# x1 transposed by DMA in 16-bit halves, attention's product moved, and a layer norm's scale folded into W1

## The chip, the cores and the metric

The kernel runs on one core of one Trainium2 chip. The metric is the device time of one execution in microseconds (us). Before the change three executions took 1932.43, 1933.75 and 1933.97 us; the median is 1933.75 us.

## What is computed

The input is src, 4 batches of 2048 rows of 256 numbers (f32). Each row is normalised (xn). Two branches work on xn, and their product is added to src.

```python
xn = layernorm(x)                                    # no scale, no shift
# branch 1: linear attention, then a two-layer network
Q, K = elu(xn @ Wq + bq) + 1, elu(xn @ Wk + bk) + 1  # 16 heads of 64
KV = einsum('bshd,bshm->bhdm', K, xn @ Wv + bv)      # sum over the rows of a batch
Z  = 1 / (einsum('bshd,bhd->bsh', Q, K.sum(axis=1)) + 1e-6)
o  = einsum('bshd,bhdm,bsh->bshm', Q, KV, Z)
x1 = layer_norm(xn + o @ Wo + bo, g1, be1)
s  = layer_norm(x1 + gelu(x1 @ W1 + b1) @ W2 + b2, g2, be2)
# branch 2: a gated network on numbers rounded to a grid of 4 bits, in blocks of 16
q  = fp4(xn)
h  = silu(q @ fp4(w_gate).T) * (q @ fp4(w_up).T)
g  = silu(fp4(h) @ fp4(w_down).T)
out = x + s * g
```

## The kernel before

**Blocks and batches.** The rows are worked on in 32 blocks of 256 rows, eight to a batch. A block's rows lie as two tiles (j) of 128 partitions. Attention of a batch needs sums over all rows of that batch (keys). They are formed one batch ahead: a prologue makes batch 0's, and the main loop (line 967) makes those of batch b + 1 while it works on the eight blocks of batch b, two portions (`subs`) per block. The first half of the portions (blocks 0 to 3 of a batch) normalises and transposes the rows; the second half reads both back from DRAM. Blocks 24 to 31, the last batch, have no keys to make.

**What one block does on TensorE.** In order, with the names that the profile shows: the product of Q (pq, `q_of`), a portion of keys (pk, `keys_k`), the sums for Z (pz, `sums`), the keys times xn (pxk, `keys_xk`), the next block's gated network (pg, `gate_up`), this block's down product (pd, `down`), the second portion of keys (pk), attention's sum (pa, `attention`), pxk of the second portion, most of the second layer of the block before (py, `ffn_2`), four transposes of x1 (pt_x, `x1_T`), one transpose of the quantiser's scales (pscale), the rest of py, and the first layer (pf, `ffn_1`). In the last batch pq stands directly ahead of pd, and a quarter of py ahead of pa.

**What sets the order.** Every product and transpose is kept in program order (`mm`, line 98, and `tr`, line 101), so TensorE works exactly in the order of the code. VectorE, ScalarE, GpSimd and SP are in program order in the prologue only; after that (`in_order[0] = False`, line 953) a planner gives each engine a fixed order ahead of the run, from program order and from when it expects operands to be ready. `tc.issue_after(ins)` puts an instruction behind another on its engine. On the chip each engine, and SP's queue of DMAs, works through its list in order and waits where an operand is missing.

**Buffers.** A tag has a fixed number of buffers, and a new tile under it waits until the tile that many places earlier is no longer read. PSUM has four buffers "mm" and two "acc". Tag "kk" has three buffers in SBUF (key products, and the transposed halves apartT), "e" three, "x1T" and "s" one each, "big" two (zq and hT).

**Two ways to transpose f32.** `transposes` (line 369) uses TensorE and an identity, and ScalarE copies the result out of PSUM. `keys_apart` (line 420) lets ScalarE split an f32 tile into its upper and lower 16-bit halves (two copies), lets one DMA transpose the 16-bit elements, and `keys_T` (line 439) joins the halves with one ScalarE copy. Before the change only keys of batches 1 to 3 are transposed in this second way; x1 goes through TensorE, and the two ScalarE instructions that evacuate it apply g1 and be1, which are constants per partition there.

**The path of Z.** `sums` writes 1/Z to DRAM (z_d) and reads it back spread over partitions (zb, four DMAs, two per half). `qz` multiplies zq with zb in two halves of four chunks; attention reads chunks 0 to 3, then 4 to 7.

**The path of the scales.** pscale is copied by ScalarE (scaleT), stored to DRAM (scale_d) and loaded into qT by eight DMAs; `quantized_h` and `quantized_x` multiply the transposed grid into qT, from which pd and pg of the next block read.

Of the kernel before, what the change touches and what calls it, by code (L numbers as in the profile page):

```python
# [15 lines left out]
P = 128  # L16
# [6 lines left out]
def linear_attention_gated_by_fp4_ffn(  # L23
# [202 lines left out]
    low = 1.5 * 2.0**22  # L226

    def fp4_scale(x, am, name):

        nb = x.shape[1]  # L230
        rs = small.tile([P, I // BLK], F32, tag="rs", name=f"rs_{name}")[:, :nb]
        vector.tensor_reduce(am, x, AX.X, ALU.max, apply_absolute_value=True)
        vector.tensor_scalar(am, am, -1.0 / 6.0, -1e-12, ALU.mult, ALU.min)
        vector.reciprocal(rs, am)
        return rs
# [144 lines left out]

    xn_d, xnT_d = {}, {}
# [38 lines left out]
    def keys_apart(b, sub, issue=None):  # L420

        f, bi = divmod(sub, NB)
        if f > 0:
            return
        n = b * NB + bi
        half = keys[b, sub][0].bitcast(U16).rearrange("p j (c f h) -> p h c j f", c=ND, h=2)
        apart = work.tile([P, 2, ND, TB, P], U16, tag="e", name=f"apart_{n}", bufs=3)
        with tc.issue_after(issue) if issue is not None else nullcontext():
            for h in range(2):
                scalar.copy(apart[:, h], half[:, h])  # L430
        apartT = work.tile([P, 2, ND * T], U16, tag="kk", name=f"apartT_{n}", bufs=3)
        nc.sync.dma_start(
            apartT.rearrange("p h (m t) -> p (h m) t", t=P),
            apart.rearrange("p h c j f -> p (h c j f)"),
            transpose=True,
        )
        keys[b, sub].append(apartT)

    def keys_T(b, sub, issue=None):

        f, bi = divmod(sub, NB)
        if f > 0:
            return
        n = b * NB + bi
        xn, *apartT = keys[b, sub]
        xnT = work.tile([P, ND, T], F32, tag="xnT_k", name=f"xnT_k_0_{n}", bufs=3)
        if apartT:
            with tc.issue_after(issue):
                scalar.copy(
                    xnT.bitcast(U16).rearrange("p c (t h) -> p h (c t)", h=2), apartT[0]  # L450
                )
        else:
            scalar.copy(xnT, transposes(xn, f"k_{n}"))
        store_xnT(n, xnT)
        keys[b, sub] = [xn, xnT]
# [59 lines left out]
    def m_of_half(b, f, dep=None, ahead=False):  # L515
# [22 lines left out]
        krow = work.tile([P, HALF], F32, tag="x1T", name=f"krow_{nm}", bufs=1)[:1, :]  # L538
# [132 lines left out]

    def gate_up(n):
# [46 lines left out]
    def q_of(n, first=None):  # L719

# [3 lines left out]
        behind = None  # L724
        for cc in range(0, NH, 2):
# [15 lines left out]
            scalar.activation(e, q1, AF.Exp, bias=neg_one)  # L741
            if first is not None and cc == 0:
                behind = first()
            with tc.issue_after(behind.ins) if behind is not None else nullcontext():
                vector.scalar_tensor_tensor(zq[:, cc : cc + 2, :], e, 1.0, q1, ALU.min, ALU.max)
# [50 lines left out]
    def x1_T(n):  # L796
        x1 = blk[n]["x1"]
        pt = transposes(x1, f"x1_{n}")
        x1T = work.tile([P, ND, T], F32, tag="x1T", name=f"x1T_{n}", bufs=1)
        for c in range(ND):  # L800
            ins = scalar.activation(
                x1T[:, c, :], pt[:, c, :], AF.Identity,
                bias=cols["be1"][:, c : c + 1], scale=cols["g1"][:, c : c + 1],
            )
        blk[n]["x1T"] = x1T
        blk[n]["act"] = ins.ins
# [145 lines left out]
    scales_h(0, 1)  # L952
    in_order[0] = False
    step(down_1)
    for sub in range(2):
        keys_in(1, sub)
    spread_scales(0, True, True)
# [4 lines left out]
    grid_T(0, 0, NCH * TB)  # L962

# [3 lines left out]
    for n in range(NBLK):  # L967
        b, bi = divmod(n, NB)
        subs = (2 * bi, 2 * bi + 1) if b + 1 < B else ()
        if n < last:  # L970
            gate = gate_up(n + 1)
        for sub in subs if n == 0 else ():
            keys_T(b + 1, sub)
        if subs:
            step(m_half)
            q_of(n)
            step(down_1)
            load_xnT(n + 1)
# [12 lines left out]
            down(n, 0)  # L991
            down(n, 1)
        elif n < last:
            def values():
                quantized_h(n, 0)
                return quantized_x(n)

            step(m_half)
            q_of(n, values)
            quantized_h(n, 1)  # L1000
            load_xnT(n + 1)
# [12 lines left out]
        if subs:  # L1014
            keys_k(b + 1, subs[1])
        elif n > 0:
            ffn_2(n - 1, 0, range(NF // 2))
        attention(n)
        if n + 2 < NBLK:
            load_xn(n + 2)  # L1020
        if subs:
# [8 lines left out]
        if n > 0:  # L1030
            ffn_2(n - 1, 0, range(0 if subs else NF // 2, NF))
            ffn_2(n - 1, 1, range(NF // 2))
        more = n + 1 < NBLK, n + 2 < NBLK
# [7 lines left out]
        for sub in next_subs[:1]:  # L1041
            keys_apart(bn + 1, sub)
        x1_T(n)
        for sub in next_subs[1:]:
            keys_apart(bn + 1, sub, blk[n]["act"])

# [7 lines left out]
        if more[0]:  # L1054
            grid_of_h(n + 1, 0)
            grid_T(n + 1, 0, NI)
            grid_of_h(n + 1, 1, blk[n]["act"])
            if more[1]:
                grid_of_x(n + 2, blk[n]["act"])
            grid_T(n + 1, NI, (NCH if more[1] else NI) * TB)  # L1060
        if n > 0:
            output(n - 1)
        if n + 1 == last:
            q_of(last)
# [44 lines left out]
```

## Time and profile before

| what | value |
|---|---|
| median of three executions | 1933.75 us |
| the profiled execution | 1931.66 us |
| its span, first to last instruction | 1929.9 us |
| TensorE, transposes of x1 (pt_x) | 128, 20.9 us busy, 277 ns mean |
| VectorE busy | 1270.7 us |
| ScalarE busy | 802.9 us |
| GpSimd busy | 534.5 us |
| granted TensorE clock, mean | 0.999 |

The busy time of a row counts each instruction from start to modelled end, and neighbouring matmuls overlap: four transposes of x1 with 277 ns each lie within about 0.6 us. What TensorE's stream really costs is read from the chain of waits, which counts each piece once. An f32 product with 256 columns stands in the trace as two matmuls and two weight loads. A "call" in the text is one product in the code, two matmuls in the trace.

Names in rows: PE is TensorE, PEld its weight loads, DVE VectorE, ACT ScalarE, POOL GpSimd, SP the engine whose queue issues the DMAs. "x<-y" says what is written from what. L99 and L102 are the helpers `mm` and `tr`, L115 the helper that records VectorE and ScalarE instructions.

### The profile page before, as it was taken

What the parts mean: (1) busy time and instruction counts of PE and PEld (TensorE: products, weight loads), DVE (VectorE), ACT (ScalarE), POOL (GpSimd) and SP (SyncE); (2) the same over time, 40 slices, a digit from 0 to 9 for tenths busy, and PEclk for the clock granted to TensorE, in tenths of its full rate; (3) what the DMA queues carried; (4) which work ended last, traced back from release to release, by engine and by line L of the source; (5) the groups of instructions that cost most, each with busy time, mean ns of one, the idle gap of its engine ahead of it and who ended that gap; (6) DMA issues with size and microseconds to landing.
All of it is one profiled execution on the core that took longest, in us unless ns stands there. A gap on an engine that the chain in (4) does not pass through costs nothing.

```text
span 1929.9 us, 22642 instructions
## 1 busy us (share of the span) xinstructions
PE 1906.7 (99%) x8020; PEld 1369.5 (71%) x8020; DVE 1270.7 (66%) x2300; ACT 802.9 (42%) x1384; POOL 534.5 (28%) x455
## 2 busy tenths in 40 slices
PE   9999999999999999999999999999999999999998
PEld 4446677667777677777677776677776777777787
DVE  7878666666566666666666666666565676677763
ACT  2334454334444355542344543454433443334442
POOL 4431232322233222322222323222232212222212
PEclk9999999999999999999999999999999999999999
DMA  4425545344434455543443554464433444444442
GB/s 153 147 93 121 111 103 113 99 107 85 93 63 94 116 100 115 127 92 96 91 87 71 114 105 102 96 124 94 100 80 73 76 81 86 81 86 82 86 85 48
DMA packets 224184, 186.99 MB, mean 97 GB/s; under 512 B 103332, under 2 KB 184768, under 8 KB 224072
## 3 DMA queue, kind: packets, MB, share of 16 engines
q1 hardware_dynamic: 223240, 183.99, 44.9%
q10 hardware_dynamic: 832, 1.57, 0.3%
q8 instruction: 63, 1.03, 0.2%
q14 instruction: 49, 0.40, 0.1%
HBM read 131.41 MB, written 31.54 MB: 84 GB/s over the span
## 4 chain that ended last, share of the span: by engine, by line
PE 84%; DMA 2%; DVE 1%; ACT 1%; SPq 1%; issue 0%; POOL 0%; POOLq 0%; DVEq 0%; ACTq 0%
PE pg L99 15%; PE py L99 11%; PE pa L99 11%; PE pf L99 10%; PE pq L99 10%; PE pxk L99 8%; PE pk L99 8%; PE pd L99 8%; PE pz L99 2%; DMA qT<-scale_d 1%; PE pt_x L102 1%; PE pm L99 1%; SPq L648 0%; DVE zq L115 0%; DMA zb<-z_d 0%
## 5 line engine op out<-in xcount | busy, mean ns | idle before, releaser
L99 PE MATMUL pg<-wgu,qT 128*128 128x352 f32 x1024 | 310.4, 461 | 0.0
L99 PEld LDWEIGHTS pg<-wgu,qT 128*128 128x128 f32 x1024 | 193.2, 190 | 118.6 <-issue 13.9
L484 POOL TENSOR_TENSOR kacc<-kacc,kk 128x512 f32<-128x512 f32 x120 | 171.2, 1427 | 304.8 <-DVE kk L115 302.7
L99 PE MATMUL pxk<-kk,xn_k 128*128 128x512 f32 x512 | 235.9, 599 | 3.4 <-DVE kk L115 3.3
L99 PE MATMUL py<-w_sb,hT 128*128 128x256 f32 x1024 | 234.4, 380 | 0.5 <-DVE s L115 0.5
L99 PE MATMUL pk<-wk_sb,xnT_k 128*128 128x512 f32 x512 | 230.4, 593 | 2.2 <-ACT xnT_k L115 1.8
L99 PE MATMUL pq<-xnT,wq_sb 128*128 128x256 f32 x1024 | 227.4, 380 | 1.6 <-ACT hT L115 1.6
L99 PE MATMUL pa<-m,zq 128*128 128x256 f32 x1024 | 227.3, 380 | 1.6 <-DVE zq L115 1.6
L99 PE MATMUL pf<-x1T,w_sb 128*128 128x256 f32 x1024 | 226.6, 379 | 0.0
L99 PEld LDWEIGHTS pa<-m,zq 128*128 128x128 f32 x1024 | 193.9, 190 | 40.1 <-issue 11.3
L99 PEld LDWEIGHTS py<-w_sb,hT 128*128 128x128 f32 x1024 | 191.0, 190 | 38.0 <-issue 8.1
L99 PEld LDWEIGHTS pq<-xnT,wq_sb 128*128 128x128 f32 x1024 | 195.2, 191 | 28.7 <-ACT hT L115 2.0
L99 PEld LDWEIGHTS pf<-x1T,w_sb 128*128 128x128 f32 x1024 | 194.3, 190 | 27.0 <-ACT hT L115 0.4
L713 POOL TENSOR_TENSOR o<-g,be_r 128x512 f32<-128x512 f32 x32 | 48.6, 1518 | 579.2 <-ACT g L115 579.2
L115 ACT ACT_TABLE_LOAD x122 | 156.5, 1283 | 96.1 <-DVE k L115 82.4
L99 PE MATMUL pd<-wd,qT 128*128 128x256 f32 x768 | 172.4, 379 | 0.1
L99 PEld LDWEIGHTS pk<-wk_sb,xnT_k 128*128 128x128 f32 x512 | 97.0, 190 | 103.8 <-issue 96.8
L99 PEld LDWEIGHTS pxk<-kk,xn_k 128*128 128x128 f32 x512 | 92.5, 190 | 109.3 <-issue 80.6
L115 DVE SCALAR_TENSOR_TENSOR zq<-e,q 128x512 f32<-128x512 f32 x128 | 86.9, 688 | 123.2 <-ACT e L115 123.1
L99 PEld LDWEIGHTS pd<-wd,qT 128*128 128x128 f32 x768 | 145.6, 190 | 24.8 <-DVE qT L115 1.3
L359 POOL TENSOR_TENSOR rstd<-rstd,neg_half 128x2 f32<-128x2 f32 (+1 forms) x97 | 72.8, 751 | 303.2 <-DVE rstd L115 259.5
L115 ACT ACTIVATE x1T<-pt_x,bcol 128x256 f32<-128x256 f32 x64 | 32.6, 560 | 257.6 <-PE pt_x L102 257.6
(123 smaller groups left out, 2337.6 us busy)
## 6 DMA issues: line engine op xcount, KB each, us to landing
zb<-z_d SPq DMA_DIRECT2D x128, 256.0 KB, 5.6
qT<-scale_d SPq DMA_DIRECT2D x248, 128.0 KB, 5.7
x_k<-in_L_attn_src_dram SPq DMA_DIRECT2D x32, 256.0 KB, 3.2
x<-in_L_attn_src_dram SPq DMA_DIRECT2D x32, 256.0 KB
xn_d<-xn_k SPq DMA_DIRECT2D x32, 256.0 KB, 3.5
xn<-xn_d SPq DMA_DIRECT2D x32, 256.0 KB, 2.5
xnT_d<-xnT_k SPq DMA_DIRECT2D x32, 256.0 KB, 4.2
xnT<-xnT_d SPq DMA_DIRECT2D x32, 256.0 KB, 2.7
```

The source lines that it names most:

```text
L99: return tc.keep_in_program_order(nc.tensor.matmul(*args, **kw))
L102: return tc.keep_in_program_order(nc.tensor.transpose(*args, **kw))
L115: ins = op(*args, **kw)
L359: nc.gpsimd.tensor_tensor(rstd[:, j0:j1], rstd[:, j0:j1], neg_half[:, j0:j1], ALU.pow)
L484: nc.gpsimd.tensor_tensor(kacc, kacc, kk, ALU.add)
L713: nc.gpsimd.tensor_tensor(o, g, rows["be2"], ALU.mult)
```

## The change

Four edits belong together.

1. x1 of blocks 1 to 30 is transposed by DMA in 16-bit halves. `apart` and `together` are the helpers of the keys, now shared. The splits follow directly on x1's normalisation, the joining copy stands where the transposes were, and is issued behind the last split that was recorded (its own, or the keys').
2. Since g1 and be1 are no longer applied to x1T, they go into the constants: W1's rows are multiplied by g1 (GpSimd), and W1's product with be1 is added to b1 (16 products with one column, in the prologue). Blocks 0 and 31 keep the transposes on TensorE, and copy them out with one instruction.
3. In blocks 1 to 23 the second portion of keys comes behind attention. In the last batch two calls of py instead of four stand ahead of pa (blocks 24 to 30).
4. For the blocks of the last batch q_of stands ahead of the first layer of the block before; q_of loads the next xnT itself. The helper that put one batch of `qT` products between q_of's VectorE instructions goes. In block 0 keys_T follows the step of `m_of_half`. krow takes the buffer "s" instead of "x1T".

```diff
+    def apart(x, name, tag, bufs):
+        half = x.bitcast(U16).rearrange("p j (c f h) -> p h c j f", c=ND, h=2)
+        xp = work.tile([P, 2, ND, TB, P], U16, tag=tag, name=f"apart_{name}", bufs=bufs)
+        for h in range(2):
+            split["last"] = scalar.copy(xp[:, h], half[:, h]).ins
+        xpT = work.tile([P, 2, ND * T], U16, tag="kk", name=f"apartT_{name}", bufs=3)
+        nc.sync.dma_start(
+            xpT.rearrange("p h (m t) -> p (h m) t", t=P),
+            xp.rearrange("p h c j f -> p (h c j f)"),
+            transpose=True,
+        )
+        return xpT
+
+    def together(xT, xpT, issue):
+        with tc.issue_after(issue):
+            return scalar.copy(xT.bitcast(U16).rearrange("p c (t h) -> p h (c t)", h=2), xpT)
...
-        krow = work.tile([P, HALF], F32, tag="x1T", name=f"krow_{nm}", bufs=1)[:1, :]
+        krow = work.tile([P, HALF], F32, tag="s", name=f"krow_{nm}", bufs=1)[:1, :]
...
+    def fold_into_w1(issue):
+        pb1 = acc_tile("pb1")
+        for c in range(NF):
+            for d in range(ND):
+                mm(
+                    pb1[:, c : c + 1], w1_sb[:, d, c * P : (c + 1) * P], cols["be1"][:, d : d + 1],
+                    start=d == 0, stop=d == ND - 1,
+                )
+        yield
+        with tc.issue_after(issue):
+            vector.tensor_tensor(cols["b1"], cols["b1"], pb1[:, :NF], ALU.add)
+        for d in range(ND):
+            nc.gpsimd.tensor_scalar(
+                w1_sb[:, d, :], w1_sb[:, d, :], cols["g1"][:, d : d + 1], None, ALU.mult
+            )
+        yield
...
-    def x1_T(n):
+    def x1_T(n, by_dma, issue=None):
+        x1T = blk[n]["x1T"] = work.tile([P, ND, T], F32, tag="x1T", name=f"x1T_{n}", bufs=1)
         x1 = blk[n]["x1"]
-        pt = transposes(x1, f"x1_{n}")
-        x1T = work.tile([P, ND, T], F32, tag="x1T", name=f"x1T_{n}", bufs=1)
-        for c in range(ND):
-            ins = scalar.activation(
-                x1T[:, c, :], pt[:, c, :], AF.Identity,
-                bias=cols["be1"][:, c : c + 1], scale=cols["g1"][:, c : c + 1],
-            )
-        blk[n]["x1T"] = x1T
-        blk[n]["act"] = ins.ins
+        if by_dma:
+            together(x1T, blk[n].pop("apart"), issue)
+        else:
+            scalar.copy(x1T, transposes(x1, f"x1_{n}"))
...
-        if subs:
+        before = 0
+        if n == 0:
             keys_k(b + 1, subs[1])
-        elif n > 0:
-            ffn_2(n - 1, 0, range(NF // 2))
+        if not subs:
+            before = NF // 4 if n < last else NF // 2
+            ffn_2(n - 1, 0, range(before))
         attention(n)
+        by_dma = 0 < n < last
+        if by_dma:
+            blk[n]["apart"] = apart(blk[n]["x1"], f"x1_{n}", "x1p", 1)
         if n + 2 < NBLK:
             load_xn(n + 2)
+        if subs and n > 0:
+            keys_k(b + 1, subs[1])
+        if n > 0:
+            ffn_2(n - 1, 0, range(before, NF))
+            ffn_2(n - 1, 1, range(NF // 2))
         if subs:
             keys_xk(b + 1, subs[1])
...
-        x1_T(n)
-        for sub in next_subs[1:]:
-            keys_apart(bn + 1, sub, blk[n]["act"])
+        x1_T(n, by_dma, split.get("last"))
...
+        if n < last and (n + 1) // NB == B - 1:
+            q_of(n + 1)
         if n > 0:
             output(n - 1)
         if n + 1 == last:
-            q_of(last)
             ffn_1(n, range(NF // 2))
```

Before the change pxk of the second portion stood directly behind pa, with py behind it; with the change pk, py and then pxk follow pa.

## The prediction

> **What bounds the kernel now.** I read the engine shares first, then the chain of work that ended last, then that chain for one ordinary block and one block of the last batch, then the single waits of TensorE.
>
> ```profile
> PE 1906.7 (99%) x8020; PEld 1369.5 (71%) x8020; DVE 1270.7 (66%) x2300; ACT 802.9 (42%) x1384; POOL 534.5 (28%) x455
> ...
> PE 84%; DMA 2%; DVE 1%; ACT 1%; SPq 1%; issue 0%; POOL 0%; POOLq 0%; DVEq 0%; ACTq 0%
> ```
>
> TensorE (PE) is the bound; beside it and its weight loads no engine exceeds 66%. So a change is worth what it takes out of PE's program-ordered stream, less what it makes that stream wait. The chain of waits for block 9 (batches 0 to 2), columns start, length, what:
>
> ```profile
> 707.68 5.18 PE pd L99 x24
> 712.86 3.43 PE pk L99 x8
> 716.30 6.91 PE pa L99 x32
> 723.20 3.43 PE pxk L99 x8
> 726.64 5.18 PE py L99 x24
> 731.82 0.44 PE pt_x L102 x4
> 732.25 0.11 PE pscale L102
> 732.36 1.73 PE py L99 x8
> 734.09 6.91 PE pf L99 x32
> ```
>
> There is no gap in it. The same view of block 26 (last batch, without keys) shows the transposes longer:
>
> ```profile
> 1687.91 3.45 PE py L99 x16
> 1691.36 0.63 PE pt_x L102 x4
> ```
>
> There they start the moment x1 is normalised, 3.64 us after the last pa, while py covers 3.45; the 0.19 us is a wait.
>
> **Part 1, the x1 transposes leave PE.** Blocks 1 to 30 lose four each: 23 x 0.44 + 7 x 0.63 = 14.5 us. In block 0 and 31 they stay. [...] Durations overlap, though: the four start 0.109 us apart, so the chain's 0.44 is what counts.
>
> In their place come rows that this kernel already has for its keys:
>
> ```profile
> L115 ACT COPY xnT_k<-apartT 128x1024 uint16<-128x1024 uint16 x22 | 29.4, 1335 | 0.0
> ...
> L115 ACT COPY apart<-xn_k 128x512 uint16<-128x512 uint16 x44 | 25.0, 617 | 89.3 <-DVE mv L115 88.7 <-DVE xn_k L115 0.6
> ...
> apartT<-apart SPq DMA_TRANSPOSE x22, 3.5
> ```
>
> ScalarE (ACT) gets 2 x 0.617 + 1.335 = 2.57 us and loses 2 x 0.56 = 1.12 us of x1T activations: +1.45 us x 30 = 44 us, at 42% busy. SP gets one transpose of 1.25 us issue time per block. Neither is on the chain if x1T arrives before ffn_1. That is the question of the whole change:
>
> Chain, from the last pa of a block: x1 normalised at +3.64 to +4.34 (all 32 blocks of the trace); two splits 1.14 (the pair overlaps a little); transpose landed 3.5 after issue (3.1 to 4.0 over the 22); joining copy 1.34; four hand-overs between engines at about 0.1. Sum 10.1 to 11.2, and I take 10.6.
>
> Cover in blocks 1 to 22, if the keys' product stands behind pa: pk 3.43, py 5.18, pxk 3.43, pscale 0.11, py 1.73 = 13.88 us (1.15 more at the two blocks of a batch that end a half of the keys). Slack 3.3 us. Without the move the cover would be 10.45 and x1T about 0.2 us late. In the last batch: 10 calls of py at 0.432, pscale 0.11, 4 more py calls 1.73, q_of 6.91 = 13.07 us, slack 2.5. Block 23 has both covers.
>
> New waits. SP's transpose of x1 waits for the splits; behind it stand stores of xn_d, loads of x_k and the keys' own transposes, then scale_d. The keys' first transpose now takes the buffer (tag kk, three of them) that x1's halves hold, so it waits for the joining copy, at about +11 instead of +8.4 (789.22 against a last pa at 780.79); its reader, the next key copy, is queued behind gelu some 8 us after ffn_1 begins, so nothing waits. In the ten blocks whose successor normalises keys, the joining copy also stands behind the last split of the keys: second key tile normalised at +8.0 (788.77), up to 2.76 later through part 2, split 1.14, copy 1.34, hand-overs 0.3: at most +13.5 against 13.88. I cost it at nothing; if that cover fails, PE waits directly.
>
> **Part 2, attention ahead of the second keys' product (blocks 1 to 23).** Eight pk instructions move behind 32 pa ones, with two additions and two min/max on VectorE (DVE; 0.685 and 0.727 us each, 2.8 us together), two exponentials and a table load on ACT (2 x 0.72 + 1.28 = 2.7) and two additions on POOL; no DMA. PE does the same work: 0 us. Two things lose cover. First, pa now follows pd at once and needs zq times Z. In the trace the first half of zq is done up to 5.0 us before pd ends and at the latest 0.8 before; the second half, needed 1.73 us into pa, is 0.18 us early in the worst block (12) and 0.53 in the next (11). Nothing, with little spare there. Second, pxk needs kk: pk ends at +3.43, addition, exponential and min/max 2.1, table load 1.3: +6.9 against +8.6. Nothing. The 2.8 us of DVE and 2.7 of ACT now fall between pa and x1T; the normalisation has idle stretches of DVE beside it (3.50 us just before, then 0.35, 0.41), so I take 1 us of delay from 0 to 2.8 for DVE and 0 to 2.0 (table load and one exponential ahead of the splits) for ACT.
>
> **Part 3, the fold.** 16 products with one column are 32 weight loads and 32 tiny matmuls. No such row exists. Below: the transposes' spacing, 0.109 x 32 = 3.5 us; above: an f32 weight load's 0.190 x 32 = 6.1 us. They stand just ahead of this:
>
> ```profile
> 150.92 0.33 PE L102 MATMUL pscale<-ident,scale 128*128 128x128 f32 x1 [4.12 <-DVE scale L115]
> ...
> 151.00:152.60 1.60, 1.60 (x10) 1.60 (x11) 1.60 (x4) 0.85 (x2) 0.53 (x1) 0.59 0.10 31
> 152.60:156.00 3.40, 3.40 (x12) 2.79 (x12) 2.79 (x6) 2.49 (x5) 0.00 (x0) 0.69 0.55 189
> ```
>
> PE sits 4.12 us there for DVE, and afterwards the granted clock (third figure from the end) is 0.59, then 0.69: 0.41 x 1.6 + 0.31 x 3.4 = 1.7 us lost. The new work fills that hole: cost -1.7 (clock held) to 6.1 - 4.1 = +2.0; I take 0. Without the hole it is 3.5 to 6.1. Scaling W1 is two POOL instructions of 1024 columns, about 2 x 1.49 = 3.0 us each by the bk row of 512 columns; POOL is idle from 152.2 to 166.0, and ffn_1 first reads W1 at 203. Nothing.
>
> **Part 4, last batch reordered.** q_of goes ahead of ffn_1, with 12 ACT instructions, 4 on DVE and one SP load (xnT, 2.7 us to landing, data stored a batch earlier). PE's work is the same. In blocks 25 to 29 pz now waits 0.41 to 0.49 us for a late zq: -2.1 us. ACT's work is the same but earlier, so gelu evacuations come later; down and pz (2.6 + 1.0 us) stand behind them. Against it, only 2 instead of 4 py calls stand before pa, 0.86 us less. VectorE's queue in block 26:
>
> ```profile
> 1677.74 1.23 DVE L115 TENSOR_TENSOR zq<-zq,zb 128x1024 f32<-128x1024 f32 x1 [1.12 <-DMA zb<-z_d]
> 1678.88 0.51 DVE L115 TENSOR_TENSOR h<-h,pg 128x352 f32<-128x352 f32 x1
> 1679.31 0.89 DVE L115 SCALAR_TENSOR_TENSOR grid<-m_h,h 128x704 bf16<-128x704 bf16 x1
> 1680.11 0.88 DVE L115 TENSOR_REDUCE scale<-h 128x44 f32<-128x704 f32 x1
> 1680.91 1.50 DVE L115 TENSOR_TENSOR zq<-zq,zb 128x1024 f32<-128x1024 f32 x1
> ```
>
> The second half ends 3.34 to 3.59 us after pd; it would be needed at 0.86 + 1.73 = 2.59, so 0.8 us late in six blocks, 4.8 us. If the planner puts it ahead of the 2.3 us between the two halves it costs nothing. I take the middle, 2.4.
>
> **Sum.** -14.5 + 0 + 0 - 2.1 + 2.4 = -14.2 us, plus 1.5 us that I allow for the places with little to spare (zq in blocks 11 and 12, the joining copy in ten blocks, gelu in the last batch): -12.7. The profiled execution took 1931.66 us (span 1929.9), 2.1 below the median of 1933.75. It becomes 1919.0, the median 1921. Own range: -14.5 - 1.7 - 2.1 = -18.3 at best, 1915; -14.5 + 2.0 + 4.8 + 2 = -5.7 at worst, 1928.
>
> **Rivals.** (a) x1T late in batches 0 to 2. With DVE and ACT delays at their upper ends the chain is 11.2 + 1.4 (half of DVE's 2.8, the rest fits its gaps) + 2.0 = 14.6, 0.7 us past the cover: x 23 = 16 us given back, median 1921 + 16 = 1937, no change to slightly slower. It turns slower from 0.55 us a block on. For it: one ACT queue carries g, table loads, exponentials and splits there. Against: ACT idles 9.87 us before the keys' splits in block 10. [...]
>
> (b) Slower: in the last batch scaleT's copy is queued on ACT behind the joining copy. Today it runs 5.9 us after pa and the next block's qT product starts just 1.1 us before pd, after DVE waited 3.53 us for that transfer; so the distance is full. Behind the joining copy it would run at +10.6, 4.7 us later, less 0.25 of longer cover and 0.3 of slack: 4.1 x 7 = 29 us, median 1950. It begins to cost from 0.55 us of delay on and outweighs the gain (12.7 / 7 = 1.8) from 2.4. For it: both stand side by side in program order, joining copy first. Against: the order is planned by readiness; today m_h, later in the program, goes ahead of scaleT (1692.94 and 1693.62).
>
> **Chances.** Forecast 0.64, (a) 0.22, (b) 0.14. What a measurement can tell from no change is 0.2%, 3.9 us. Faster 0.65 (the forecast and 0.01 of (a)), same 0.10 (of (a)), slower 0.25 (0.11 of (a) and (b)). Range 1915 to 1938: the forecast's own 1915 to 1928 and (a), leaving (b) and a little of (a) out.
>
> **What would show it.** Right: pt_x x8 in place of x128; chain of waits of block 9 from pa through pk, py, pxk, pscale, py to pf without gap, one block 57.3 instead of 57.75 us; the hole at 150.92 filled. Wrong: waits of pf for ACT x1T (a), waits of pd or pg for qT after block 23 (b), waits of pa for zq over 1 us (part 4).

## The result and the profile after

The changed kernel takes 1992.46 us in the median of six runs (1989.45 to 1997.39); the kernel before, beside it on the same chip, 1934.05 us (six runs, 1932.43 to 1937.24). The ratio is 1.0302 with a 95% interval of 1.0286 to 1.0317: 58 us slower, where 13 us faster was forecast. The profiled execution took 1994.05 us. Its page, engines first, then the shares of the chain that ended last, then two groups of TensorE (busy us, mean ns, idle us before them and what ended it):

```profile
PE 1919.6 (96%) x7932; PEld 1366.2 (69%) x7932; DVE 1363.1 (68%) x2301; ACT 842.6 (42%) x1411; POOL 554.0 (28%) x457
...
PE 59%; DVE 14%; DMA 8%; POOL 4%; ACT 2%; issue 2%; SPq 1%; POOLq 0%; DVEq 0%; ACTq 0%
...
L99 PE MATMUL pxk<-kk,xn_k 128*128 128x512 f32 x512 | 237.7, 603 | 15.1 <-DVE kk L115 14.9
...
L99 PE MATMUL pd<-wd,qT 128*128 128x256 f32 x768 | 185.7, 400 | 23.7 <-DVE qT L115 19.6
```

TensorE executes 88 instructions less, and yet its share of the chain falls from 84% to 59%; VectorE, DMA and GpSimd have taken over. VectorE has the same number of instructions (2301 against 2300) and is busy 92 us longer: the same work has become slower. The start of pf in each block splits the span into three stretches:

| stretch | before, us | after, us | difference |
|---|---|---|---|
| start to the first pf | 203.33 | 204.99 | +1.7 |
| pf of block 0 to pf of block 22 | 1293.72 | 1317.66 | +23.9 |
| pf of block 22 to the end | 432.80 | 469.61 | +36.8 |

**Batches 0 to 2.** Where no new wait appears, a block takes 57.32 us instead of 57.75: the forecast 0.44 us is there. But ten blocks (1, 2, 7 to 10, 15 to 18), those whose successor normalises keys, take 0.9 to 2.2 us more than before, and so do blocks 3, 11, 12 and 19 (0.9 to 2.3 us). (A block is counted here from the pf of the block ahead to its own.) The chain of waits of block 9 after the change, columns start, length, what:

```profile
735.75 0.70 POOL rstd L360
736.45 0.03 issue
736.48 2.69 DVE xn_k L115 x2
739.17 0.16 DVE mv L115 x2
739.32 0.59 DVE kk L115
739.91 0.07 issue
739.98 1.64 POOL kacc L491
...
741.73 0.71 POOL rstd L360
...
742.46 1.66 DVE xn_k L115 x2
744.12 0.10 DVE scale L115
744.23 1.12 ACT apart_k L115 x2
745.35 1.26 ACT x1T L115
...
746.65 3.50 PE pf L99 x15
```

Before, this block's chain was TensorE from end to end. Now it runs through the normalisation of the next keys (rstd, xn_k), kk, GpSimd's kacc, the second keys' xn_k, their split, and only then the copy of x1T, because that copy is queued behind the last split. x1T is there 16.34 us after the last pa; TensorE had 13.88 us of work. TensorE doesn't lose all of that at pf: it waits in three places of this block, and the wait for x1T is the shortest.

```profile
739.95 3.70 PE L99 MATMUL pxk<-kk,xn_k 128*128 128x512 f32 x8 [0.92 <-DVE kk L115]
744.27 0.33 PE L102 MATMUL pscale<-ident,scale 128*128 128x128 f32 x1 [0.62 <-DVE scale L115]
746.65 7.17 PE L99 MATMUL pf<-x1T,w_sb 128*128 128x256 f32 x32 [0.32 <-ACT x1T L115]
```

From the pf of block 0 to that of block 22 such waits sum to 11.7 us ahead of pxk, 5.9 ahead of pks (the sums over kacc, at the end of a half of the keys: blocks 3, 11 and 19), 5.0 ahead of pscale and 2.6 ahead of pf. Before the change there were none of these. The timeline of block 9 shows why xn_k takes 2.69 us for two instructions:

```profile
736.41 1.26 POOL L826 TENSOR_TENSOR x<-x,g_r 128x512 f32<-128x512 f32 x1
736.48 2.69 DVE L115 TENSOR_SCALAR xn_k<-x_k,mv,rstd 128x256 f32<-128x256 f32 x2 [0.48 <-POOL rstd L360]
737.75 1.26 POOL L827 TENSOR_TENSOR x<-x,shift_r 128x512 f32<-128x512 f32 x1
```

Each of the two ends 0.15 us after an instruction of GpSimd, x1 times g1 (the first) and plus shift (the second). Before the change the same two GpSimd instructions came after TensorE's transposes of x1, which they overwrite. In block 9 before the change both xn_k pairs were done by then:

```profile
730.27 0.73 DVE L115 TENSOR_SCALAR xn_k<-x_k,mv,rstd 128x256 f32<-128x256 f32 x2 [0.66 <-POOL rstd L359]
733.30 1.27 POOL L808 TENSOR_TENSOR x<-x,g_r 128x512 f32<-128x512 f32 x1
```

In the whole trace 1 of 64 xn_k overlaps one of the two GpSimd instructions before the change, and 21 after it. In block 9 it is this overlap that delays kk, not GpSimd's own queue: GpSimd was done with the two at 739.01 us and idle until kk came. In blocks 3, 11 and 19 GpSimd's queue is the way: there the second kacc, which pks waits for, stands right behind plus shift.

**The last batch.** Timeline around block 27, SPq being SP's queue of DMAs. First SP's queue in block 26 before the change:

```profile
1693.91 0.32 SPq L645 DMA_DIRECT2D scale_d<-scaleT  x1
1695.48 3.63 SPq L648 DMA_DIRECT2D qT<-scale_d  x8
1699.21 1.47 SPq L657 DMA_TRANSPOSE gridT<-grid  x1
```

and after it, with the other engines:

```profile
1728.93 0.27 PE L102 MATMUL pscale<-ident,scale 128*128 128x128 f32 x1
...
1731.50 0.33 SPq L652 DMA_DIRECT2D scale_d<-scaleT  x1
...
1734.05 1.33 SPq L664 DMA_TRANSPOSE gridT<-grid  x1
...
1735.49 3.95 SPq L655 DMA_DIRECT2D qT<-scale_d  x8
...
1746.44 2.43 DVE L115 TENSOR_TENSOR qT<-qT,gridT 128x768 f32<-128x768 f32 x3 [4.89 <-DMA qT<-scale_d]
...
1747.50 5.46 PE L99 MATMUL pd<-wd,qT 128*128 128x256 f32 x12 [3.62 <-DVE qT L115]
```

The eight loads of qT now stand behind the second transpose of gridT, which waits for VectorE's grid. The store of the scales to DRAM begins 2.57 us after pscale (1.22 before), the loads begin 1.4 us after gridT's transpose, and pd waits 3.62 us. Then the twelve pd behind the wait take 5.46 us, where they took 2.7 before. Windows of the same stretch (sums per engine; the third figure from the end is the granted TensorE clock):

```profile
1747.40:1750.00 2.60, 2.50 (x6) 2.08 (x7) 1.47 (x2) 0.00 (x0) 0.00 (x0) 0.50 0.00 0
```

The clock granted after the idle time is 0.50. So this wait of 3.62 us costs 6.4 in all (3.62 + 5.46 - 2.7).

### The profile page after: what moved, and what is told of

The parts are those of the page before. It is cut to its first block, busy times and chain, and to the rows that moved or that the text cites. A ratio compares the mean times of both kernels' runs of the same rounds, so it can differ in the third digit from the quotient of the medians.

```text
span 1992.3 us, 22613 instructions
## 1 busy us (share of the span) xinstructions
PE 1919.6 (96%) x7932; PEld 1366.2 (69%) x7932; DVE 1363.1 (68%) x2301; ACT 842.6 (42%) x1411; POOL 554.0 (28%) x457
## 4 chain that ended last, share of the span: by engine, by line
PE 59%; DVE 14%; DMA 8%; POOL 4%; ACT 2%; issue 2%; SPq 1%; POOLq 0%; DVEq 0%; ACTq 0%
PE pg L99 10%; PE pf L99 9%; PE pq L99 9%; PE pa L99 8%; PE pd L99 7%; PE pxk L99 6%; PE pk L99 5%; PE py L99 4%; DMA zb<-z_d 3%; DVE xn_k L115 2%; PE pz L99 1%; DVE x L115 1%; POOL rstd L360 1%; POOL kacc L491 1%; DMA qT<-scale_d 1%
## 5 line engine op out<-in xcount | busy, mean ns | idle before, releaser
L99 PE MATMUL pxk<-kk,xn_k 128*128 128x512 f32 x512 | 237.7, 603 | 15.1 <-DVE kk L115 14.9
L99 PE MATMUL pd<-wd,qT 128*128 128x256 f32 x768 | 185.7, 400 | 23.7 <-DVE qT L115 19.6
L99 PEld LDWEIGHTS pd<-wd,qT 128*128 128x128 f32 x768 | 154.1, 202 | 53.0 <-issue 25.6
L115 ACT ACTIVATE m_h<-h 128x704 bf16<-128x704 f32 x64 | 50.5, 790 | 264.1 <-DVE h L115 264.1
L115 ACT ACTIVATE h<-pg 128x352 f32<-128x352 f32 x128 | 58.7, 459 | 237.5 <-PE pg L99 237.5
```

What stands on the lines that cost most here:

```text
L99: return tc.keep_in_program_order(nc.tensor.matmul(*args, **kw))
L115: ins = op(*args, **kw)
```

## The experiments

All times are medians; ratios are to the kernel before, run beside them. "0 to 22" and "22 on" are the second and third stretch of the table above (before: 1293.72 and 432.80 us), from the one profiled execution of each run. Runs e1 to e10 were made on one chip, e11 to e14 on a second and e15 and e16 on a third, so between these groups the ratios compare better than the times.

| run | us | ratio, 95% interval | 0 to 22 | 22 on |
|---|---|---|---|---|
| e1_qt_first | 1957.89 | 1.0126 (1.0107 to 1.0145) | 1317.33 | 436.14 |
| e2_pool_late | 1950.25 | 1.0086 (1.0068 to 1.0103) | 1291.98 | 451.08 |
| e3_keys_first | 1993.31 | 1.0308 (1.0292 to 1.0323) | 1319.61 | 472.12 |
| e4_last_as_before | 1996.41 | 1.0320 (1.0305 to 1.0336) | 1319.27 | 474.38 |
| e5_both | 1929.26 | 0.9979 (0.9970 to 0.9989) | 1291.68 | 432.09 |
| e6_no_affine | 1947.42 | 1.0074 (1.0059 to 1.0089) | 1291.77 | 448.28 |
| e9_last_full | 1956.32 | 1.0124 (1.0107 to 1.0141) | 1313.73 | 435.59 |
| e10_full_pool | 1930.26 | 0.9986 (0.9977 to 0.9996) | 1292.02 | 432.68 |
| e11_x1_first | 1925.19 | 0.9960 (0.9948 to 0.9973) | 1287.34 | 432.36 |
| e12_x1_first_py4 | 1925.29 | 0.9962 (0.9949 to 0.9974) | 1286.99 | 432.90 |
| e13_by_pe | 1931.70 | 0.9993 (0.9984 to 1.0002) | 1293.23 | 432.45 |
| e14_keys_first | 1931.76 | 0.9996 (0.9987 to 1.0005) | 1294.14 | 432.01 |
| e15_scale_early | 1923.04 | 0.9953 (0.9940 to 0.9967) | 1285.38 | 433.62 |
| e16_last_pe | 1925.98 | 0.9967 (0.9955 to 0.9980) | 1286.65 | 432.12 |

The first pf starts between 203.1 and 207.1 us over these runs, though none of them changes the prologue; differences of 2 us there mean nothing.

### The order of two entries on SP's queue

```diff
+            with tc.issue_after(loaded["last"].ins) if n + 2 > (B - 1) * NB else nullcontext():
-            grid_T(n + 1, NI, (NCH if more[1] else NI) * TB)
+                grid_T(n + 1, NI, (NCH if more[1] else NI) * TB)
```

> The changed kernel, with one thing moved: in the last batch the second transpose of gridT, which stands ahead of the eight loads of qT on SP's queue and waits there for DVE's grid, goes behind them. Of the 58 us lost, the block intervals lay some 35 us in the last batch. Theory 1: the loss there is the load of qT, late by SP's order, and the clock that falls to about 0.5 after the idle time. Then the waits ahead of pd shrink from 3.9-4.7 us to about 1.4 us, the twelve pd behind them take about 2.8 us again instead of 5.5, and the time falls by some 5.2 us in each of six blocks, about 31 us, to about 1961 us. Rival 2: scaleT itself and DVE's product on qT are late (their queue on ACT), so the order on SP changes little: 1985 us or more. In between, if the wait shrinks but the clock still falls behind a shorter wait: about 1977 us.

34.6 us went, nearly all from the last stretch (469.61 to 436.14), more than the theory's 31. The timeline of a block there:

```profile
1722.12 3.63 SPq L656 DMA_DIRECT2D qT<-scale_d  x8
1725.86 1.43 SPq L665 DMA_TRANSPOSE gridT<-grid  x1
1732.67 2.53 DVE L115 TENSOR_TENSOR qT<-qT,gridT 128x768 f32<-128x768 f32 x3 [1.68 <-DMA qT<-scale_d]
...
1733.73 2.83 PE L99 MATMUL pd<-wd,qT 128*128 128x256 f32 x12 [0.40 <-PE pf L99]
```

The wait is down to 0.40 us, and the twelve pd take 2.83 us; the mean clock granted in this execution is 0.998, in the changed kernel's 0.990. Rival 2 falls as the main cause. What it named is still seen: scaleT is copied 2.2 and 2.3 us after pscale in two blocks (1.2 in the four others), and pd's two longest waits of this stretch, 1.06 and 1.14 us, follow these two.

### GpSimd's two operations on the residual, moved and left out

```diff
-        nc.gpsimd.tensor_tensor(x1, x1, rows["g1"], ALU.mult)
-        nc.gpsimd.tensor_tensor(x1, x1, rows["shift"], ALU.add)
...
             output(n - 1)
+            if n < last:
+                with tc.issue_after(power["last"]):
+                    x1_rows(n)
```

> The changed kernel, with POOL's two operations on the residual (x1 times g1, plus shift) moved on POOL's queue behind the rstd of the block before, so that they don't run while DVE normalises the next keys. Theory 1: DVE's operations with two SBUF operands and its TENSOR_SCALAR are stretched while POOL's tensor operations run (xn_k 402 ns alone, 1373 ns beside them); that, and kacc behind them on POOL, is what delays kk, pxk, the last split and x1T in batches 0 to 2. Then the ten blocks whose successor normalises keys lose their extra 2.2 us, the four at a half's end some of their 1.3 to 2.3 us, and the time falls by 20 to 25 us to about 1970 us. Rival 2: the moved keys' product or the added copies do it, whatever POOL does: 1987 us or more. It may also move the collision to another stretch: then DVE's time beside POOL stays as long and the time falls by less than 10 us.

> The changed kernel without POOL's two operations on the residual in blocks 1 to 30: x1 times g1 and the added shift are left out there, everything else and SP's order stay. Theory: DVE's operations are stretched by POOL's tensor operations beside them. Then xn_k falls from a mean of some 980 ns to under 450 ns and grid<-m_x from 940 to under 500 ns, with the same operands; DVE's busy time falls by some 80 us or more; the waits for kk, and of pks, go; in batches 0 to 2 each block takes what the best ones take now (57.3 us), and the last batch keeps some of its wait for qT, since gridT's transpose still stands ahead of the loads. Time: about 1945 us, near that of the run with the two operations moved. Rival: DVE's instructions are long because of something else that stands beside them (PSUM, DMA writes to SBUF); then their means stay within 15% and the time above 1980 us.

Moving them took 42 us off, leaving them out 45. In both, 26 us went from batches 0 to 2, as the theory had it, and 18 to 21 us from the last batch, which it hadn't separated. There the transpose of gridT that holds up the loads of qT goes out 5.0 to 5.1 us after pscale in the changed kernel and 3.6 to 3.7 us with the operations moved. It waits for grid, and in each of the blocks 24 to 29 something ahead of it on VectorE is stretched: in four blocks y, which takes 1.75 to 1.81 us (0.69 with the operations moved), in the two others grid itself, 2.31 us for two instructions (0.74 moved). Groups of VectorE in the changed kernel:

```profile
L115 DVE TENSOR_SCALAR xn_k<-x_k,mv,rstd 128x256 f32<-128x256 f32 x64 | 60.2, 980 | 12.7 <-POOL rstd L360 12.7
L115 DVE SCALAR_TENSOR_TENSOR grid<-m_x,y 128x256 bf16<-128x256 bf16 x64 | 55.6, 908 | 0.9
...
L115 DVE SCALAR_TENSOR_TENSOR o<-s,rstd,o 128x256 f32<-128x256 f32 x64 | 28.3, 482 | 18.7 <-POOL rstd L360 18.7
```

and in the run with the operations moved:

```profile
L115 DVE SCALAR_TENSOR_TENSOR o<-s,rstd,o 128x256 f32<-128x256 f32 x64 | 88.8, 1424 | 18.7 <-POOL rstd L362 18.7
...
L115 DVE SCALAR_TENSOR_TENSOR grid<-m_x,y 128x256 bf16<-128x256 bf16 x64 | 36.6, 611 | 0.9
L115 DVE TENSOR_SCALAR xn_k<-x_k,mv,rstd 128x256 f32<-128x256 f32 x64 | 31.3, 531 | 24.7 <-POOL rstd L362 24.7
```

xn_k is back at 531 ns, and now it is o that takes 1424 ns in place of 482. VectorE's busy time hardly moves (1363.1 to 1357.3 us), as the third case of the expectation had it, but the conclusion drawn there was wrong: in batches 0 to 2 the collision costs next to nothing where it is now (1291.98 us, against 1291.77 with the operations left out; in the last batch the two runs are 2.8 us apart). With the operations left out xn_k takes 530 ns, grid 610, o 481 and VectorE is busy 62 us less; the expectation had said under 450, under 500 and 80 us or more. GpSimd's other operations still collide: grid from m_h keeps its mean of 1242 ns (1243 in the changed kernel, where the 36 of 64 with no GpSimd tensor operation beside them take 883 and the 24 beside one for half their time or more 1842).

### Both

> The changed kernel with both single edits, gridT's second transpose behind the loads of qT in the last batch, and POOL's two operations on the residual behind the rstd of the block before. Alone, the first took 34.6 us off (all of it in blocks 23 to 30), the second 42.3 us (some 25 us in batches 0 to 2, the rest in the last batch). If both act on the same wait in the last batch, the sum there isn't more than the wait: the waits ahead of pd of 2.6-3.5 us that the second alone left go as they did with the first, and the time is 1992.5 - 42 - (6 x 3) = about 1930 to 1936 us. If the two are independent: 1992.5 - 34.6 - 42.3 = 1915.6 us. If POOL's operations, moved, hold back something else: above 1945 us.

1929.26 us, just under the first of the three cases: the two causes act on one wait in the last batch, whose stretch is back at 432.09 us. This is 0.2% under the kernel before, with an interval of 0.1 to 0.3%.

### The last batch as it was

```diff
-        by_dma = 0 < n < last
+        by_dma = 0 < n < (B - 1) * NB
...
-            before = NF // 4 if n < last else NF // 2
+            before = NF // 2
...
+            q_of(n)
             quantized_h(n, 0)
...
-        if n < last and (n + 1) // NB == B - 1:
-            q_of(n + 1)
+        if n + 1 == last:
+            q_of(last)
```

> The changed kernel with the last batch as before: x1 of blocks 24 to 31 transposed by PE again, q of a block directly ahead of its pd, four of the quantised products ahead of pa; batches 0 to 2 as in the changed kernel. Theory 1: the losses of the two stretches are separate, so this takes the last batch's 35 us away and leaves those of batches 0 to 2: about 1957 us, with no wait for qT ahead of pd. Rival 2: the lateness comes from the earlier batches' queues and is carried on: above 1975 us.

Nothing went; both theories' numbers were missed. The timeline shows a wait of the same size from another place (VectorE, then TensorE):

```profile
1751.25 0.69 DVE L115 SCALAR_TENSOR_TENSOR zq<-e,q 128x512 f32<-128x512 f32 x1 [0.79 <-ACT e L115]
...
1751.86 2.42 DVE L115 TENSOR_TENSOR qT<-qT,gridT 128x768 f32<-128x768 f32 x3
...
1752.87 5.49 PE L99 MATMUL pd<-wd,qT 128*128 128x256 f32 x12 [3.68 <-DVE qT L115]
```

The loads were issued by 1740.06 us, but the product on qT stands behind four zq. In the kernel before, a helper put the product ahead of them, and the grids were held behind x1T; the change dropped both orders. The next run restores them as well.

```diff
+            def values():
+                quantized_h(n, 0)
+                return quantized_x(n)
-            q_of(n)
-            quantized_h(n, 0)
-            quantized_x(n)
+            q_of(n, values)
...
+            if first is not None and cc == 0:
+                behind = first().ins
+            with tc.issue_after(behind) if first is not None else nullcontext():
...
-            grid_of_h(n + 1, 1)
+            grid_of_h(n + 1, 1, act)
```

> The changed kernel with the whole last batch as it was before the change: as the run that put back PE's transposes, q_of's place and four quantised products, and besides the two orders that the change dropped there, the products on qT between q_of's operations on VectorE, and the grids held behind the copy of x1T. That other run kept waits of 3.8 us ahead of pd, and its timeline shows the product on qT on VectorE behind all four zq, though the loads were issued at 1736 us. Theory: that order, and nothing carried over from earlier batches, is the cause; then no wait for qT is left and the time is that run's less the last batch's 35 us: about 1958 us. Rival: something else of the change, W1 folded or POOL's order, makes the last batch slow: above 1975 us.

> The last batch wholly as before, and in blocks 1 to 23 POOL's two operations on the residual behind the rstd of the block before. Theory: the time of the run before less 25 us in batches 0 to 2: 1930 to 1935 us, which would say that the changed kernel's loss is these two places, and that of the gain forecast for the transposes (14.5 us) only some 2 us is left after POOL's and the copies' waits. Rival: the two edits interfere (POOL's operations moved make the first blocks of the last batch late): above 1942 us. If the gain forecast were all there: 1920 us.

1956.32 and 1930.26 us, as the theories said. pd has no wait for qT left. Two hand-written orders, in lines that look like bookkeeping, carry as much as the whole loss of the last batch (e4 and e9: 474.38 and 435.59 us; no run restores one of the two alone). The version with q_of moved reaches the same with the order on SP's queue in their place (e1).

### What the transposition and the move are worth

```diff
-        by_dma = 0 < n < last
+        by_dma = False
```

> The run with both edits, but x1 of all blocks transposed by PE, so that the orders and the folded W1 stay and the transposition alone goes back. The forecast's first part put the transposes at 23 x 0.44 + 7 x 0.63 = 14.5 us. If they are worth that, where nothing waits instead, this takes 1929 + 14.5 = 1943 to 1944 us. If the new waits for x1T (0.48 us in ten blocks) are counted against it: 1938 us. If the transposes' time was hidden anyway: 1929 us. In the blocks that took 57.32 us it should be 57.75 us again.

```diff
-        if n == 0:
-            keys_k(b + 1, subs[1])
+        if subs:
+            keys_k(b + 1, subs[1])
         attention(n)
...
-        if subs and n > 0:
-            keys_k(b + 1, subs[1])
```

> The changed kernel with one part undone: the second keys' product stands in front of attention again, x1 still goes through DMA in 16-bit halves. Theory 1: the move is what gives x1T its cover; without it PE has about 10.5 us of work between the last pa and pf where x1T needs 10.6 us when it isn't delayed and 13 to 16 us where the keys' splits stand ahead of the copies. Then pf waits 1 to 4 us for x1T in most of 23 blocks: 2000 to 2030 us. Rival 2: the move itself brings POOL and DVE into collision, and undoing it takes the 2.2 us of ten blocks away: about 1970 us. No change (1990 to 1995 us) would mean that the move neither costs nor covers anything.

> The run with both edits, but the second keys' product back in front of attention, so that x1T's cover loses pk's 3.4 us: some 10.5 us of PE's work against a chain of 10.6 us and more. The earlier run of this order, without the two edits, was as fast as the changed kernel: pf waited 21 us for x1T, and the waits for kk fell from 13.6 to 3.4 us. Theory: with POOL's operations moved there is nothing of the keys' side to win, and pf's waits alone remain: 10 to 20 us slower than 1929, 1939 to 1949 us. Rival: the waits for x1T were POOL's doing too, and the move covers nothing: 1928 to 1932 us.

With all transposes back on TensorE the kernel takes 1931.70 us, 2.4 more than with both edits (the intervals of the two ratios touch), below every number expected but the last. Its ordinary blocks take 57.75 us again, so 0.44 us per block is real; but seven blocks that take 0.4 to 0.5 us more than before in e5 (2, 8 to 10, 16 to 18) take as long as before here, and the last stretch is as long (432.45 and 432.09). The order with keys first, e3, came out unchanged, by two amounts that cancel: pf waits 21.1 us for x1T instead of 2.6, and pxk waits 3.3 us for kk instead of 14.9. My expectation's reading of "no change", that the move neither costs nor covers, was wrong. With GpSimd's operations moved (e14), the second amount isn't there, and keys first costs 2.5 us in batches 0 to 2, not the 10 to 20 expected: x1T is ready after 9.7 to 11.9 us against 10.45 to 11.55 of cover, so pf waits in about half of the blocks, 7.3 us in all.

### Toward a kernel faster than both

In e5 ten blocks still have x1T only 14.69 us after the last pa, behind the second keys' split.

```diff
-        for sub in next_subs:
+        for sub in next_subs[:1]:
             keys_apart(bn + 1, sub)
         x1_T(n, by_dma, split.get("last"))
+        for sub in next_subs[1:]:
+            keys_apart(bn + 1, sub, blk[n]["act"])
```

(The first keys' split stays ahead of x1_T; `act` is the copy of x1T.)

> The run with both edits, and x1T's joining copy put ahead of the second split of the keys on ScalarE, as the order was before the change. In that run pf still waits 0.48 us for x1T in ten blocks (the copy stands behind the split, which waits for VectorE and POOL), and those blocks take 58.28 us where the others take 57.32. Theory: the copy's operand is there by then, so the wait goes: 10 x 0.48 = 4.8 us, 1924 to 1925 us; pscale's wait of 0.32 us stays. Rival: the copy then waits for the DMA itself, or the keys that stand behind it are late in the next block (pk waits for xnT_k): 1928 us or more.

1925.19 us: x1T is ready after 10.3 to 11.1 us in these blocks and no wait of pf for it is left. Of the 4.8 us expected 4.1 came; in e5 pf had waited in eight of the ten blocks.

```diff
-            before = NF // 4 if n < last else NF // 2
+            before = NF // 2
```

> The kernel of the run before it in this call, and in the last batch four calls of py ahead of pa in place of two, as before the change. pa waits there 0.6 to 1.2 us for the second half of zq in each of seven blocks. Theory: two more calls (0.9 us) hide most of that, and x1T's cover behind pa shrinks from 13.1 to 11.2 us, which the chain of 10.6 us still fits: 4 to 5 us faster than the run before it, 1919 to 1921 us. Rival: x1T is then late and pf waits instead, no faster or slower.

A miss: 1925.29 us. pf doesn't wait, and pa's waits do shrink, from 4.1 to 1.6 us, but the last stretch stays (432.36 and 432.90): pd waits 4.2 us instead of 2.5, and pscale, which didn't wait in the last batch, now waits about 0.2 us in five blocks.

> The run of 1925.2 us with x1 of blocks 24 to 30 transposed by PE. The forecast put those seven transposes at 0.63 us each, 4.4 us. In the run with all transposes on PE the last batch took as long as in the run with none (its blocks 45.06, 44.90, 44.88, 44.88, 44.87 us against 45.46, 44.57, 45.31, 44.88, 44.50). Theory: in the last batch the transposes' time goes into the wait of pa for zq's second half, which starts that much earlier and ends where it did, so putting them back costs nothing: 1924.5 to 1926 us. Rival: they are worth what was forecast: 1929 to 1930 us.

The outcome was as the theory said (1925.98, last stretch 432.12), the mechanism not quite: pa waits 4.1 us for zq in e11 and 4.4 here, hardly more. What goes in return for the transposes is pd's wait, 2.5 us in e11 and 0.1 here.

```diff
-        for sub in next_subs if n > 0 else ():
+        for sub in next_subs[:1] if n > 0 else ():
             keys_in(bn + 1, sub)
...
-        for sub in next_subs if n == 0 else ():
+        for sub in next_subs[1:] if n > 0 else next_subs:
             keys_in(bn + 1, sub)
```

> The run of 1925.2 us (both edits, x1T's copy ahead of the second keys' split), with the second portion of keys normalised behind the quantiser's scale in program order. In that run pscale waits 0.31 us in ten blocks: DVE's scale stands behind xn_k, which waits 1.4 us for POOL's rstd, which stands behind two kacc on POOL. Theory: the chain from kacc over rstd and xn_k to scale is the rest of what those blocks lose; with scale ahead they take 57.32 us in place of 57.67: 3.5 us faster, 1921 to 1922 us. Rival: the keys, now later, are late in the next block (pk waits for xnT_k, pxk for kk), or the collision with kacc falls on another DVE instruction of the chain: 1924 us or more.

1923.04 us, 0.9953 of the kernel before and the fastest of the study. The ordinary blocks take 57.32 us, and of the ten, blocks 2, 9, 10, 17 and 18 now do too (57.66 to 57.69 in e11). Blocks 8 and 16 got slower instead (61.00 and 60.84 us, 60.66 and 60.63 in e11): there pg waits 0.45 to 0.58 us for qT. The chain of waits of one of the five (block 10) is TensorE's alone again, now without pt_x:

```profile
767.30 6.91 PE pa L99 x32
774.21 3.43 PE pk L99 x8
777.64 5.18 PE py L99 x24
782.82 3.43 PE pxk L99 x8
786.25 0.11 PE pscale L102
786.36 1.73 PE py L99 x8
788.09 6.91 PE pf L99 x32
```

In the 22 intervals from block 0 to 22 that makes 8.3 us less than before; 22 x 0.44 would be 9.7. Against e11 the interval of the ratio overlaps; the stretches (1287.34 and 1285.38) are what says that the edit worked.

## Why the prediction was wrong

12.7 us less were forecast and 58 us more came: 24 in batches 0 to 2, 37 in the last batch. In each of the two stretches a wait failed that the sum has at nothing; the gain from the transposes is there in the first and not in the second.

**Part 1, the size of the gain: right where it was reached.** 0.44 us per block in batches 0 to 2 is what 57.75 against 57.32 us shows, and e13 gives it back. The chain to x1T, taken as 10.6 us, is 10.3 to 10.8 in most blocks where nothing stands in its way, about 9.4 in the last batch; the covers of 13.88 and 13.07 are 13.88 and 13.06. For the last batch 7 x 0.63 us was wrong: e16 puts the transposes back at no cost, since without them (e11) pd waits 2.5 us for qT that it doesn't wait with them.

**Part 1, the first step that failed.** "In the ten blocks ... at most +13.5 against 13.88. I cost it at nothing." It was +16.34. The term that was too small is the second key tile, "+8.0, up to 2.76 later through part 2", so +10.8 at most. In the changed kernel that tile is normalised at +13.9 and in e5, where the two GpSimd operations are out of the way, at +12.2. What is left in e5 is seen on GpSimd's queue (block 10):

```profile
786.80 3.02 POOL L495 TENSOR_TENSOR kacc<-kacc,kk 128x512 f32<-128x512 f32 x2 [1.58 <-DVE kk L115]
789.79 0.70 POOL L362 TENSOR_TENSOR rstd<-rstd,neg_half 128x2 f32<-128x2 f32 x1
790.52 0.73 DVE L115 TENSOR_SCALAR xn_k<-x_k,mv,rstd 128x256 f32<-128x256 f32 x2 [1.43 <-POOL rstd L362]
```

The tile's rstd stands behind the two kacc of the moved product. Part 2 lists these as "two additions on POOL" and gives them no time; with keys first (e14) they run ahead of pa, and the tile is at +8.0. So the orders alone make x1T's +14.69 (e5), and GpSimd beside VectorE makes the other 1.65. Rival (a) had x1T late for this sort of reason, but put it 0.7 us past the cover in all 23 blocks; it was 2.5 us in eight of them.

**Part 2, "PE does the same work: 0 us", and kk: "+6.9 against +8.6. Nothing."** The first kk came at +9.6, so pxk waited, and these waits (11.7 us) are the largest of batches 0 to 2. The prediction counted what the moved product issues. It didn't count what the removed transposes had been holding back: GpSimd's x1 times g1 and plus shift. They now start as soon as the splits have read x1, beside the next keys' xn_k, and kk stands behind xn_k; with the two moved (e5) the first kk comes at +7.7 and pxk doesn't wait. The price was in the profile of before: there, too, the group of xn_k has a mean of 530 ns, though 50 of the 64 have no GpSimd tensor operation beside them and take 409 (median). e2 and e6 show that these two instructions, by when they run, cost 26 us in batches 0 to 2, through VectorE in most blocks and through GpSimd's queue in blocks 3, 11 and 19.

**Part 3, the fold: right as far as it can be seen.** The 16 products took 3.63 us and stand in the hole; pscale's wait there is 0.34 us in place of 4.12. W1's scaling takes GpSimd 2.94 us per instruction (3.0 estimated). The hoped-for clock isn't held: it is 0.87 and then 0.56 in the two windows. No run leaves the fold out, and the first stretch varies by more than its price.

**Part 4, "PE's work is the same": the second step that failed.** The late zq ahead of the end of pz is gone, as forecast, and was worth more than the 2.1 us put for it: pz took 1.65 to 1.73 us in five blocks and takes 1.00 there in e5, 3.4 us in all. pa waits 4.9 us for zq instead of 1.6, so 3.3 where 2.4 was put. What failed is the term that isn't there: the distance from pscale to pd, called full in rival (b), was priced only for ScalarE's queue. The loss came on SP's, where the planner put gridT's transpose ahead of the loads: they begin 6.4 to 6.6 us after pscale in all six blocks, whether scaleT was copied 1.2 us after pscale or 2.2 to 2.3. GpSimd's two operations make that transpose later still (5.0 to 5.1 us after pscale, 3.6 to 3.7 with them moved), and the clock (0.50 behind the wait of block 27) made a wait of 4 us one of 6 to 7. e1 (order alone: 33.5 us of this stretch), e2 (GpSimd alone: 18.5) and e5 (37.5) show that both feed one wait. Rival (b) had the place, the symptom and nearly the size (29 us), at a chance of 0.14, but not the cause: scaleT runs ahead of the joining copy (1731.23 and 1732.46 us in block 26), so that the size came out near is luck.

What remains open: why the planner changed the order on SP's queue. The grids are no longer held behind x1T's copy, which may be why, but no run restores that order alone; the planner works ahead of the run from its own estimates, and no run here looks into them.

## What to carry to other kernels

When an instruction leaves, ask what it was holding back as well as what it cost: its readers and overwriters start earlier, and where two engines slow each other, as here (xn_k takes 402 ns alone and 1373 beside GpSimd), earlier can mean beside the wrong neighbour. When a kernel has hand-written orders and a planner beside them, compare the queues (SP's too) entry by entry before trusting "same work, other place". And a longer busy time is no cost in itself: e2 has VectorE as busy as the changed kernel and is 42 us faster, because the slow instruction (o, 1424 ns in place of 482) is now one that TensorE hardly waits for.

## What the runs showed of the hardware

**VectorE beside GpSimd.** In the changed kernel's trace 20 of 64 xn_k have no GpSimd tensor operation beside them and take 402 ns (median); 38 run beside one for half their time or more and take 1373 ns (mean); the other six overlap one by less than 0.2 us and take 402. grid from m_x takes 418 alone and 1339 beside one. k<-pk,bk, which reads one operand from PSUM, takes 684 and 683; the statistics of x (418 and 419) and the reduction of h (882 and 878) don't change either. Which of the two starts first matters for kk. It takes 682 ns (mean) alone; the 21 that start before the GpSimd operation beside them take 679, and the 25 that start after it 1544 (overlaps under 0.1 us left out). GpSimd's operation takes 1.27 us alone (median) and 1.68 (mean) where kk started first, so there GpSimd's operation is the one that takes longer. The product on qT (128x512), which starts first 17 times, takes 684 in these. (xn_k fits less neatly: ten stretched ones start within 8 ns of the GpSimd operation, one starts 0.2 us ahead of it.) In e2, where the two GpSimd operations stand behind the rstd that o waits for, o takes 1424 ns in place of 482.

**The clock after a wait.** Counted from start to start, all thirteen waits ahead of pd of 4.0 us and more in the changed kernel and in e4 were followed by a slower TensorE: twelve pd took 4.05 to 5.42 us instead of 2.7 (granted clock in windows behind four of the six in the changed kernel: 0.50, 0.68, 0.50, 0.50). Of the six waits of 2.8 to 3.7 us in e2 two were (4.15 and 4.45 us), four not (2.76), and the two were not the longest. The granted clock falls to 0.50 and 0.52 behind the two (2.89 and 3.05 us) and is 1.00 in the windows taken behind three of the four others, 3.64 and 3.74 us among them: between 2.8 and 3.7 us the length alone does not decide in this run. After the shorter waits in e1, 0.5 to 1.5 us, twelve pd took 2.83 us at most.
